# Where the value product stands in an attention kernel: from a fixed two windows behind to wherever a window has room

## The chip, the core and the metric

The kernel runs on one core of a Trainium2 chip. The metric is the time of one execution on the device in microseconds (us); lower is better. Beside the times there is one profiled execution, whose trace gives the start and length of every instruction on each engine: TensorE (PE; its weight loads are listed apart as PEld), VectorE (DVE), ScalarE (ACT), GpSimd (POOL), and SyncE (SP), which issues the DMAs.

## The reference, cut to what matters

```python
def attn(x, Wq, Wk, Wv, Wo):                 # x: 8 x 1024 x 256
    H, G, THETA = 16, 4, 10000.0             # 16 query heads, 4 key heads
    q, k, v = x @ Wq, x @ Wk, x @ Wv
    ...
    scores = jnp.einsum('bhqd,bhkd->bhqk', q, k) / jnp.sqrt(jnp.float32(D))
    p = jax.nn.softmax(scores, axis=-1)
    o = jnp.einsum('bhqk,bhkd->bhqd', p, v)
    return o.transpose(0, 2, 1, 3).reshape(B, S, D) @ Wo

x = x + layernorm(attn(layernorm(x), Wq, Wk, Wv, Wo))
x = x + layernorm(ternary_ffn(layernorm(x)))
```

Queries and keys are rotated by position (RoPE) between the projection and the scores. The feed-forward layer is one product with weights rounded to -1, 0 or 1.

## The kernel before

**Units, groups, blocks.** The work is cut into 16 units of 512 queries (half a sequence). A unit has 4 groups of 4 heads. For a group the keys come in 8 key tiles of 128. A key tile with the 4 heads of a group is a step: four exp scores, one for each head, each 128 keys by 512 queries. So there are 512 steps and 2048 exp scores, counted by `s`. One exp score is one score product into a PSUM bank (`se`, three of them, line 655) and one exp on ACT into an SBUF tile of the pool `ep` (line 671). That pool has 12 tiles. Ahead of that, 13 steps earlier, a second pass over the same scores finds each query's maximum: two score products into a two-bank PSUM tile (`sm`, two of them, line 582), then a maximum over 1024 numbers on DVE (line 607), which may be taken as two halves.

**The value product.** `av_piece` (line 691) multiplies the exp tiles of a key tile with the values and adds up over a group in the one PSUM bank `av`. It works in blocks of 128 query columns, so a key tile has 4 blocks, and there are 2048 blocks, as many as exp scores. A piece is a run of blocks inside one key tile. It costs four weight loads and four matmuls, one for each head, and each 32-bit matmul shows as two instructions in the trace, hence the "x8" there. When a group is finished, `av_out` copies the bank to an SBUF tile of the pool `avp` (5 tiles; ACT, line 704) and sends it to DRAM (`d_av`, line 712).

**Windows.** TensorE, VectorE and ScalarE run an order written out by hand. `window(s)` emits one window: 3 exp scores, or 2 where a part of other work with a PSUM bank of its own is waiting, each beside a score product for the maxima; then the parts that have come due (`do_parts`, at most one banked part in a window of 2, none in a window of 3); then value products. `behind` holds the windows whose value product is still to come, and `av_windows(2)` issues as many blocks as the window two places back had exp scores. So every window ends with 2 or 3 blocks, whatever else it holds. A piece needs all four exp tiles of its key tile.

**Other work.** `P_PARTS` lists by step what projects a later unit (norm, transposes `x`, key and value product `kv_and_dram`, query products `q`, and DMAs through DRAM), `T_PARTS` what follows attention for the unit before (`fetch` of the value products from DRAM, `invert` of the softmax denominators on DVE, `scale` on GpSimd, output product `attn`, feed-forward `ffn`, norms). `P_FIRST` and `T_LAST` replace the steps for the first such unit and the last but one. The DMAs of all of these go through the one queue of SP, in program order; there a DMA that waits holds up those behind it.

Of the kernel before, what the change touches and what calls it, by code (L numbers as in the profile page):

```python
# [16 lines left out]
P = 128  # L17
H = 16
HKV = 4
G = H // HKV  # L20
# [8 lines left out]
def kernel(  # L29
# [35 lines left out]
    NK = S // P  # L65
    UPB = S // UQ
    NU = B * UPB
    NROW = 3 * HD
    SPU = G * NK
    NSTEP = NU * SPU  # L70
    LEAD, START = 13, 10

    const = ctx.enter_context(tc.tile_pool(name="const", bufs=1))
# [1 line left out]
    small = ctx.enter_context(tc.tile_pool(name="small", bufs=4))  # L75
    work = ctx.enter_context(tc.tile_pool(name="work", bufs=2))
    qkp = ctx.enter_context(tc.tile_pool(name="qkp", bufs=1))
    ep = ctx.enter_context(tc.tile_pool(name="ep", bufs=12))
    avp = ctx.enter_context(tc.tile_pool(name="avp", bufs=5))
    tailp = ctx.enter_context(tc.tile_pool(name="tailp", bufs=1))  # L80
    dram = ctx.enter_context(tc.tile_pool(name="dram", bufs=3, space=DRAM))
    ps_mx = ctx.enter_context(tc.tile_pool(name="ps_mx", bufs=2, space=PSUM))
# [110 lines left out]
    ffn = {}  # L193
# [424 lines left out]
    sm, mhl, shifts, reduced, early = {}, {}, {}, [], [None]  # L618
# [30 lines left out]
    es, av_ps, av_sb, d_av = {}, {}, {}, {}  # L649
# [33 lines left out]
    def av_piece(i, first, end):  # L683

        va = v_aug[(i // G // UPB) % 3]
        if first == 0:
            av_ps[0] = ps_av.tile([P, UQ], F32, tag="av", name=f"av_{i}")
        for kt in range(first // UQ, (end - 1) // UQ + 1):
            lo, hi = max(first - kt * UQ, 0), min(end - kt * UQ, UQ)
            for r in (1, 2, 3, 0):  # L690
                nc.tensor.matmul(  # L691
                    av_ps[0][32 * r : 32 * r + 32, lo:hi],
                    va[:, kt, r, :],
                    es[i * NK + kt, r // 2, r % 2][:, lo:hi],
                    start=(kt == 0 and lo == 0),
                    stop=(kt == NK - 1 and hi == UQ),
                )

    def av_out(i):

        u, j = divmod(i, G)
        a = av_sb[u, j] = avp.tile([P, UQ], F32, tag="avsb", name=f"avsb_{i}")
        if i < NU * G - 1:
            nc.scalar.copy(a, av_ps[0])
        else:
            half = UQ // 2
            nc.scalar.copy(a[:, :half], av_ps[0][:, :half])
            nc.vector.tensor_copy(a[:, half:], av_ps[0][:, half:])
        if u < NU - 1:
            if j == 0:  # L710
                d_av[u] = dram.tile([H, 32, UQ], F32, tag="d_av", name=f"d_av_{u}")
            nc.sync.dma_start(out=d_av[u][HKV * j : HKV * (j + 1)], in_=a)


    class Tail:
# [21 lines left out]

        def fetch(self):

            for c in range(2):  # L740
                self.on[c] = self.new("xn", c)
                nc.sync.dma_start(
                    out=self.on[c].rearrange("p t d -> p (t d)"),
                    in_=d_av[self.u][8 * c : 8 * c + 8, 0:HD, :],
                )
            self.den = small.tile([P, UQ // 8], F32, tag="den", name=f"den_{self.u}", bufs=1)
            nc.sync.dma_start(
                out=self.den, in_=d_av[self.u][:, HD, :].rearrange("i (g t) -> i g t", g=8)
            )
# [88 lines left out]
    class LastTail(Tail):  # L838
# [55 lines left out]
        x = o  # L894
# [42 lines left out]
    def load(u):  # L937
# [2 lines left out]


    P_PARTS = (
        (26, "begin", 0), (33, "x", 0, 0), (34, "x", 0, 1), (37, "begin", 1), (43, "x", 1, 0),
        (45, "x", 1, 1), (49, "kv_and_dram"), (51, "q", 0), (52, "kt"), (53, "v"), (55, "q", 1),
        (57, "q_to_dram"),
    )
    L_PARTS = (
        (10, "n", 0), (13, "o", 0), (15, "attn", 0), (16, "stats_a", 0), (19, "stats_x", 0),
# [2 lines left out]
        (29, "attn", 2), (29, "x", 1), (30, "stats_a", 2), (30, "ffn", 1), (31, "stats_f", 1),  # L951
    )
    T_PARTS = (
        (1, "fetch"), (7, "invert"), (8, "scale", 0), (9, "scale", 1), (12, "attn", 0),
        (15, "attn", 1), (15, "stats_a", 0), (17, "stats_a", 1), (19, "stats_x", 0),
        (23, "stats_x", 1), (24, "x", 0, 0), (25, "x", 0, 1), (26, "ffn", 0), (27, "x", 1, 0),
        (29, "x", 1, 1), (31, "ffn", 1), (31, "stats_f", 0), (33, "stats_f", 1),
    )

    P_FIRST = (47, 51, 52, 54, 57, 58, 59, 60, 62, 61, 63, 64)  # L960
    T_LAST = (1, 3, 4, 5, 9, 10, 11, 14, 17, 20, 21, 21, 22, 24, 25, 26, 23, 27)

    warm = []

# [15 lines left out]
    def behind_shift(i, f, *args):  # L980

        with tc.issue_after(shifts[i]):
            f(*args)

    for k, fs in enumerate((
        [second("x", 1, 0), second("x", 1, 1), second("kv", 0)],
        [second("kv", 1), (pick, "q", 0, 0, 1), (pick, "q", 0, 1, 1), second("v"),
         second("rotate_k"), second("split_k")],
        [(pick, "q", 1, 0), (keep_warm, 1)],
        [(keep_warm, 3), second("k"), (keep_warm, 4), (pick, "k", 1, 0), (pick, "k", 1, 1),  # L990
         (keep_warm, 2)],
        [(pick, "q", 1, 1), second("q_product", 0), third("stats", 0),
         third("norm", 0, nc.scalar)],
        [second("q_product", 1), third("stats", 1), third("hi", 0, nc.scalar), third("lo", 0),
         (pick, "q", 2, 0)],
        [(pick, "q", 2, 1), third("norm", 1, nc.scalar), third("hi", 1, nc.scalar),
         third("lo", 1), (keep_warm, 3), (fill_constant_parts, 1)],
        [third("x", 0, 0), (pick, "q", 3, 0), (keep_warm, 3)],
        [third("x", 0, 1), (pick, "q", 3, 1), second("rotate_q", 0), (keep_warm, 2)],
        [third("x", 1, 0), third("x", 1, 1), second("split_q", 0)],  # L1000
        [third("kv_and_dram"), second("rotate_q", 1)],
        [third("v"), second("split_q", 1), second("q_to_dram")],
        [],
        [],
        [(fill_constant_parts, 2)],
        [],
        [third("q", 0)],
        [(behind_shift, 1, third("kt"))],
        [third("q", 1), (behind_shift, 1, stack_queries, 1)],
        [third("q_to_dram")],  # L1010
    )):
        for f in fs:
            at(k - START, *(f if isinstance(f, tuple) else (f,)))
    for u in range(3, NU):
        start = SPU * (u - 4)
        steps = P_FIRST if u == 3 else [k for k, *_ in P_PARTS]
        at(start + steps[0] - 6, load, u)
        if u == 3:
            for k, stage in (
                (7, measure), (9, prepare_wo), (11, add_up), (13, threshold), (15, ternarize),  # L1020
                (22, transpose_ternary),
            ):
                at(k, stage)
        at(start + steps[0] - 1, begin_project, u)
        for k, (_, *p) in zip(steps, P_PARTS):
            at(start + k, part, projects, u, *p)
    for u in range(2, NU):
        at(SPU * (u - 1) + 1, stack_queries, u)
    for u in range(NU - 1):
        start = SPU * (u + 1)  # L1030
        at(start + 1, begin_tail, u)
        steps = [k for k, *_ in T_PARTS] if u < NU - 2 else T_LAST
# [14 lines left out]
        )  # L1047

    REGULAR = 40
    ends = 4 * (NSTEP - LEAD)  # L1050


    ready = []
# [22 lines left out]

    def do_parts(banks):

        while ready:
            f, args = ready[0]  # L1080
            if banked(f, args):
                if banks == 0:
                    break
                banks -= 1
            ready.pop(0)
            f(*args)
            if f is shift_rows:
                split_later.append(args[0])

    def take_low():  # L1090
        while split_later:
# [8 lines left out]
        collect(n)  # L1100
        do_parts(99)

    behind, done, split_later = [], [], []

    def av_windows(lag):

        while len(behind) > lag:
            i, s, size = behind.pop(0)
            first = s % (4 * NK)
            av_piece(i, first * P, (first + size) * P)  # L1110
            if first + size == 4 * NK:
                done.append(i)

    def window(s):


        late, size = s >= ends, window_size(s)
        if done:
            av_out(done.pop())
        if late:  # L1120
            for r2 in range(2):
                exp_two(s // 4, r2)
        else:
            end = min(maxima_by(s + size), 4 * NSTEP)
            for q in range(max(size, end - maxima[0])):
                if q < size:
                    exp_one(s + q)
                if maxima[0] < end:
                    max_scores(maxima[0])
                    maxima[0] += 1  # L1130
                if q == 0:
                    take_low()
            reduce_early(maxima[0])
        take_low()
        behind.append((s // (4 * NK), s, size))
        for n in range(s // 4, (s + size) // 4):
            collect(n)
        do_parts(3 - size if REGULAR <= s < ends else 99)
        av_windows(1 if late else 2)
        return s + size  # L1140

    E = mybir.EngineType
    due, picks = [], []
# [56 lines left out]
    with tc.manual_schedule(engines={E.PE, E.DVE, E.Activation}):  # L1200
        while s < 4 * NSTEP:
            s = window(s)
        av_windows(0)
        av_out(NU * G - 1)
        assert not (todo or due or ready or split_later)
# [70 lines left out]
```

## Time and profile before

| | us |
|---|---|
| median of 3 runs (1644.11 to 1649.19) | 1645.35 |
| profiled execution, its own time | 1642.63 |
| its span, first to last instruction | 1640.8 |

The timeline can be cut into windows: from the first score matmul of one to the first score matmul of the next. Between 105 and 1573 us there are 751, together 1468.8 us. Sorted by what they hold besides scores and value products:

| window (exp scores; part) | windows | all, us | mean length, us | mean blocks | DVE idle in all, us |
|---|---|---|---|---|---|
| light: 3; none | 438 | 791.2 | 1.806 | 2.61 | 97.5 |
| transposes: 2; `x` of either list | 109 | 216.2 | 1.983 | 2.63 | 28.9 |
| heavy: 2; `attn` (31) | 31 | 92.6 | 2.989 | 2.55 | 25.5 |
| heavy: 2; `q` (26) | 26 | 83.8 | 3.225 | 2.50 | 8.4 |
| heavy: 2; `ffn` (28) | 28 | 71.4 | 2.552 | 2.00 | 2.2 |
| heavy: 2; `kv_and_dram` (13) | 13 | 41.8 | 3.212 | 3.00 | 2.8 |
| shift: 2; transpose of the maxima `pm` | 61 | 100.9 | 1.655 | 2.52 | 1.6 |
| rest: 2; small parts or none | 45 | 70.9 | 1.576 | 2.62 | 11.9 |

In the timeline a line gives start, length, engine, line of the kernel, operation, tiles and shape, how many instructions were merged (x8), and in brackets how long the engine had been idle and what ended it. The length of a matmul contains its way through the array, so what a group of matmuls costs the engine is read from its start to the start of the next group.

### The profile page before, as it was taken

The numbers are of one execution on the slowest core, as the hardware profiler recorded it, in microseconds if no ns is written. First come the engines' busy times: TensorE is split into PE (matmuls) and PEld (weight loads), VectorE is DVE, ScalarE is ACT, GpSimd is POOL, SyncE is SP. The second block draws the span as 40 slices with busy tenths as digits, with TensorE's granted clock in tenths as the row PEclk, the third lists the DMA queues.
The fourth block names the chain that finished last, engine by engine and source line by source line (L and its number), as shares of the span: only waits on it lengthen the run. The fifth ranks groups of instructions, "written<-read, shape, count | busy, mean of one in ns | idle before, by whom it ended". The sixth has DMA issues, their size and how long they took to land.

```text
span 1640.8 us, 37250 instructions
## 1 busy us (share of the span) xinstructions
PE 1579.7 (96%) x14712; PEld 818.5 (50%) x14712; DVE 1399.3 (85%) x2049; ACT 1274.8 (78%) x2479; POOL 835.4 (51%) x1239
## 2 busy tenths in 40 slices
PE   7999999999999999999999999999999999999997
PEld 5544455454545545454544545455454544444544
DVE  7778788889898888989889898988989888898964
ACT  4657778878787887878788787887878787877884
POOL 5532457374653737455373835547374552323363
PEclk8989999999999999999999999999999999999999
DMA  4151425125151422515133251513325151231100
GB/s 139 53 101 34 91 77 101 59 76 101 56 106 49 91 67 82 101 46 105 60 83 75 77 106 44 104 49 89 71 67 104 40 97 42 46 70 34 42 15 27
DMA packets 86079, 117.99 MB, mean 72 GB/s; under 512 B 12088, under 2 KB 50808, under 8 KB 85752
## 3 DMA queue, kind: packets, MB, share of 16 engines
q1 hardware_dynamic: 85904, 115.60, 29.9%
q8 instruction: 116, 1.90, 0.5%
q14 instruction: 59, 0.48, 0.1%
HBM read 68.65 MB, written 45.88 MB: 70 GB/s over the span
## 4 chain that ended last, share of the span: by engine, by line
PE 80%; DVE 10%; DMA 3%; ACT 2%; POOL 2%; issue 2%; SPq 1%; POOLq 0%; DVEq 0%; ACTq 0%
PE av L691 28%; PE se L655 28%; PE sm L582 9%; DVE mx L607 7%; PE pa L283 3%; PE pq L283 2%; PE pf L283 2%; PE pt_ot L267 2%; ACT e L671 2%; PE pt_xt L267 2%; PE pkv L283 2%; DMA q_st<-ml 1%; DMA k_rot<-d_k 1%; PE pm L630 1%; DMA dk<-ks 1%
## 5 line engine op out<-in xcount | busy, mean ns | idle before, releaser
L607 DVE TENSOR_REDUCE mx<-sm 128x2 f32<-128x1024 f32 (+1 forms) x1304 | 1205.3, 973 | 191.9 <-PE sm L582 174.1
L671 ACT ACTIVATE e<-se 128x512 f32<-128x512 f32 x1996 | 1058.2, 602 | 223.0 <-PE sm L582 172.4
L582 PE MATMUL sm<-k_st,q_st 64*128 64x512 f32 x2048 | 748.4, 450 | 6.9 <-DVE mx L607 3.9
L655 PE MATMUL se<-q_st,k_st 64*128 64x512 f32 x2048 | 705.5, 441 | 26.7 <-ACT e L671 14.4
L691 PE MATMUL av<-e,v_aug 128*32 128x256 f32 (+3 forms) x8608 | 607.2, 378 | 0.0
L655 PEld LDWEIGHTS se<-q_st,k_st 64*128 64x128 f32 x2048 | 324.9, 185 | 405.7 <-ACT e L671 302.1
L582 PEld LDWEIGHTS sm<-k_st,q_st 64*128 64x128 f32 x2048 | 326.1, 185 | 65.1 <-DVE mx L607 41.9
L691 PEld LDWEIGHTS av<-e,v_aug 128*32 128x32 f32 x8608 | 194.4, 108 | 211.0 <-issue 148.3
L241 POOL TENSOR_SCALAR lnsc<-mv 128x2 f32<-128x2 f32 (+1 forms) x134 | 25.8, 193 | 400.1 <-DVE mv L239 395.1
L765 POOL TENSOR_TENSOR xn<-xn,a 128x512 f32<-128x512 f32 x30 | 38.4, 1282 | 131.8 <-DMA a<-d_rec 101.2
L826 POOL TENSOR_TENSOR a<-a,bias_bc 128x512 f32<-128x512 f32 x30 | 38.6, 1287 | 108.3 <-ACT a L825 108.3
L242 POOL TENSOR_TENSOR lnsc<-lnsc,mhalf 128x2 f32<-128x2 f32 (+1 forms) x134 | 92.5, 691 | 0.9
L162 POOL TENSOR_TENSOR hl<-xn,hl 128x512 fp32r<-128x512 f32 x60 | 76.5, 1287 | 0.4
L253 POOL TENSOR_SCALAR xn<-x,lnsc 128x256 f32<-128x256 f32 x116 | 65.1, 570 | 2.2
L237 DVE BATCH_NORM_STATS2 bnst<-a 128x6 f32<-128x256 f32 x120 | 44.5, 413 | 4.6 <-POOL a L826 4.6
L297 POOL TENSOR_TENSOR t<-q_rot,sin_q_sb 128x512 f32<-128x512 f32 x31 | 39.9, 1288 | 15.5 <-ACT q_rot L439 15.4
L283 PE MATMUL pa<-woh,hl 128*128 128x256 f32 x240 | 46.2, 294 | 1.1 <-ACT e L671 1.1
L283 PE MATMUL pq<-xt,wqkvh 128*128 128x256 f32 x256 | 45.8, 303 | 0.5 <-ACT e L671 0.5
L237 DVE BATCH_NORM_STATS2 bnst<-x 128x6 f32<-128x256 f32 x124 | 45.9, 412 | 0.4 <-DMA x<-in_L_attn_x 0.4
L271 ACT CAST ot<-pt_ot 128x512 fp32r<-128x512 f32 x66 | 39.6, 601 | 4.7 <-PE pt_ot L267 4.7
L439 ACT COPY q_rot<-pq 128x512 f32<-128x512 f32 x32 | 18.8, 586 | 30.9 <-PE pq L283 30.9
L162 POOL TENSOR_TENSOR hlq<-q_rot,hlq 128x512 fp32r<-128x512 f32 x31 | 39.8, 1285 | 4.8 <-ACT hlq L159 4.5
(157 smaller groups left out, 1303.1 us busy)
## 6 DMA issues: line engine op xcount, KB each, us to landing
q_st<-dq SPq DMA_DIRECT2D x90, 256.0 KB
dq<-hlq SPq DMA_DIRECT2D x60, 256.0 KB
d_av<-avsb SPq DMA_DIRECT2D x60, 256.0 KB
x<-in_L_attn_x SPq DMA_DIRECT2D x15, 512.0 KB
xn<-d_av SPq DMA_DIRECT2D x30, 256.0 KB
a<-d_rec SPq DMA_DIRECT2D x30, 256.0 KB
xr<-in_L_attn_x SPq DMA_DIRECT2D x15, 512.0 KB
out_x<-a SPq DMA_DIRECT2D x30, 256.0 KB
```

Source lines behind the costliest of these rows:

```text
L162: eng.tensor_tensor(lo, src, hi.bitcast(F32), ALU.subtract)
L237: nc.vector.bn_stats(st[:, t, :], src[:, t, :])
L242: nc.gpsimd.tensor_tensor(sc[:, 1, :], sc[:, 1, :], mhalf[:, :n], ALU.pow)
L253: eng.tensor_scalar(dst[:, t, :], src[:, t, :], sc[:, 0, t : t + 1] if eng is nc.gpsimd else mv[:, t, 0:1], sc[:, 1, t : t + 1], ALU.add i ...
L267: nc.tensor.transpose(pt[:, c, t * P : (t + 1) * P], src[:, t, c * P : (c + 1) * P], ident_r)
L283: nc.tensor.matmul(out, chunk(left[i], c), chunk(right[j], c), start=(k == 0), stop=(k == len(steps) - 1),)
L297: eng.tensor_tensor(dst, x, table.unsqueeze(1).to_broadcast(list(x.shape)), ALU.mult)
L582: scores = nc.tensor.matmul(sm[0][:, part, :], queries[rows], k_st[(u // UPB) % 3][rows, r2, ch * 512 : (ch + 1) * 512], start=True, stop= ...
L607: early[0] = nc.vector.tensor_reduce(mx[i][:, a, head_and_tile(i, r2, t), lo:n], sm[0][:, lo:n, :], AX.X, ALU.max).ins
L655: nc.tensor.matmul(sc if len(queries.shape) == 2 else sc.rearrange("p (j t) -> p j t", j=G), k_st[(i // G // UPB) % 3][rows, r2, kt * P : ...
L671: nc.scalar.activation(e, sc, AF.Exp, scale=1.0 / D**0.5)
L691: nc.tensor.matmul(av_ps[0][32 * r : 32 * r + 32, lo:hi], va[:, kt, r, :], es[i * NK + kt, r // 2, r % 2][:, lo:hi], start=(kt == 0 and lo ...
```

## The change

The value product is no longer issued at a fixed distance. `behind` and `av_windows` are gone. A counter `av_at` tells how many blocks are done, and at the end of every window `av_end` chooses how far to go: it tries each end up to 8 blocks on, inside the group, and takes the one whose weight (that of the banked parts just issued, plus 21 for each block and 6 for each piece) comes closest to 95, with 45 added for an end inside a key tile. It goes no further than the key tiles whose exps were emitted before this window, and no less far than `least`, which 16 exp tiles need. When the group ends, `av_out` follows in the next window as before.

With it go: 16 exp tiles for 12 and 2 output tiles for 5; `fetch` two steps later; several project parts up to five steps later, and the DMAs of `kt` and `q_to_dram` held behind the latest DMA of shift rows; for the last but one unit `fetch`, `invert` and both `scale` two steps later. A window's number of exp scores, its parts and the order inside it are as before.

```diff
+    E_TILES = 16
-    ep = ctx.enter_context(tc.tile_pool(name="ep", bufs=12))
-    avp = ctx.enter_context(tc.tile_pool(name="avp", bufs=5))
+    ep = ctx.enter_context(tc.tile_pool(name="ep", bufs=E_TILES))
+    avp = ctx.enter_context(tc.tile_pool(name="avp", bufs=2))
...
     P_PARTS = (
-        (26, "begin", 0), (33, "x", 0, 0), (34, "x", 0, 1), (37, "begin", 1), (43, "x", 1, 0),
-        (45, "x", 1, 1), (49, "kv_and_dram"), (51, "q", 0), (52, "kt"), (53, "v"), (55, "q", 1),
-        (57, "q_to_dram"),
+        (30, "begin", 0), (35, "x", 0, 0), (36, "x", 0, 1), (37, "begin", 1), (43, "x", 1, 0),
+        (45, "x", 1, 1), (49, "kv_and_dram"), (51, "q", 0), (54, "kt"), (53, "v"), (55, "q", 1),
+        (62, "q_to_dram"),
     )
...
     T_PARTS = (
-        (1, "fetch"), (7, "invert"), (8, "scale", 0), (9, "scale", 1), (12, "attn", 0),
+        (3, "fetch"), (7, "invert"), (8, "scale", 0), (9, "scale", 1), (12, "attn", 0),
...
-    T_LAST = (1, 3, 4, 5, 9, 10, 11, 14, 17, 20, 21, 21, 22, 24, 25, 26, 23, 27)
+    T_LAST = (3, 5, 6, 7, 9, 10, 11, 14, 17, 20, 21, 21, 22, 24, 25, 26, 23, 27)
...
+    def behind_latest(f, *args):
+
+        behind_shift(max(shifts), f, *args)
...
-        at(start + steps[0] - 1, begin_project, u)
-        for k, (_, *p) in zip(steps, P_PARTS):
-            at(start + k, part, projects, u, *p)
+        first = 25 if u == 4 else steps[0]
+        at(start + first, begin_project, u)
+        for k, (_, *p) in zip([first + (u == 4), *steps[1:]], P_PARTS):
+            behind = [behind_latest] if p[0] in ("kt", "q_to_dram") else []
+            at(start + k, *behind, part, projects, u, *p)
...
+    GAP, COLUMNS, PIECE, SPLIT = 95, 21, 6, 45
+    WEIGHT = {"x": 46, "v": 33, "ffn": 112, "q": 162, "attn": 162, "kv_and_dram": 162}
...
+    def av_end(s, size, weight):
+
+
+
+        at = av_at[0]
+        least = (s + 3 - E_TILES + 3) // 4 * 4
+        then = (s - 1) // 4 * 4
+        best = None
+        for end in range(at, min(at + 8, at // (4 * NK) * 4 * NK + 4 * NK) + 1):
+            if end > max(at, least) and (end + 3) // 4 * 4 > s - size - 1:
+                break
+            pieces = (end + 3) // 4 - at // 4 if end > at else 0
+            rest = abs(weight + COLUMNS * (end - at) + PIECE * pieces - GAP)
+            rest += SPLIT * (end % 4 > 0) + 1000 * max(0, least - end)
+            if not ready and end > at and end == then:
+                rest += 80
+            if best is None or rest < best[0]:
+                best = rest, end
+        return best[1]
...
-        behind.append((s // (4 * NK), s, size))
         for n in range(s // 4, (s + size) // 4):
             collect(n)
-        do_parts(3 - size if REGULAR <= s < ends else 99)
-        av_windows(1 if late else 2)
-        return s + size
+        weight = do_parts(3 - size if REGULAR <= s < ends else 99)
+        s += size
+        av_until(s - 4 if late else av_end(s, size, weight))
+        return s
```

`do_parts` now returns the summed weight of the banked parts it issued (those of `WEIGHT`, 30 for another part, 25 for the shift rows' transpose and the like), and `av_until(end)` issues the blocks from `av_at` to `end` by `av_piece`.

More of the change, by code (lines that the diff above doesn't have):

```diff
@@ L738, in fetch @@
         def fetch(self):
+            assert (self.u, G - 1) in av_sb
             for c in range(2):
@@ L1077, in do_parts @@
     def do_parts(banks):
+        weight = 0
         while ready:
@@ L1084, in do_parts @@
                 banks -= 1
+                weight += WEIGHT.get(args[2], 30) if f is part else 25
             ready.pop(0)
@@ L1088, in do_parts @@
                 split_later.append(args[0])
+        return weight
     def take_low():
@@ L1101, in start_step, with av_until @@
         do_parts(99)
[L1103 to L1111, printed above, removed]
-                done.append(i)
+    done, split_later, av_at = [], [], [0]
+    def av_until(end):
+        i, first = divmod(av_at[0], 4 * NK)
+        last = min(end - i * 4 * NK, 4 * NK)
+        if last > first:
+            av_piece(i, first * P, last * P)
+            av_at[0] += last - first
+            if last == 4 * NK:
+                done.append(i)
+    def av_end(s, size, weight):
[14 more added lines that the diff above has]
+        return best[1]
     def window(s):
@@ L1202 @@
             s = window(s)
-        av_windows(0)
-        av_out(NU * G - 1)
-        assert not (todo or due or ready or split_later)
+        av_until(s)
+        av_out(done.pop())
+        assert av_at[0] == s and not (todo or due or ready or split_later or done)
     spare[0] = 1
```

## The prediction

> **What bounds the kernel now.** I read the page first: the engines' shares and the costliest groups.
>
> ```profile
> PE 1579.7 (96%) x14712; PEld 818.5 (50%) x14712; DVE 1399.3 (85%) x2049; ACT 1274.8 (78%) x2479; POOL 835.4 (51%) x1239
> ...
> L607 DVE TENSOR_REDUCE mx<-sm 128x2 f32<-128x1024 f32 (+1 forms) x1304 | 1205.3, 973 | 191.9 <-PE sm L582 174.1
> L671 ACT ACTIVATE e<-se 128x512 f32<-128x512 f32 x1996 | 1058.2, 602 | 223.0 <-PE sm L582 172.4
> ...
> L691 PE MATMUL av<-e,v_aug 128*32 128x256 f32 (+3 forms) x8608 | 607.2, 378 | 0.0
> ```
>
> PE looks full and DVE waits mostly for PE, but a busy matmul is not PE at its peak. So I went to the sums by stretch (length; then busy time and instructions of PE, PEld, DVE, ACT, POOL; clock, DMA share, GB/s): a window with an `attn` part, a light one, the steady state.
>
> ```profile
> 602.72:605.58 2.86, 2.86 (x29) 1.95 (x25) 1.29 (x2) 1.64 (x4) 0.00 (x0) 1.00 0.02 6
> ...
> 608.74:610.59 1.85, 1.85 (x19) 0.82 (x15) 1.85 (x4) 1.85 (x5) 0.00 (x0) 1.00 0.00 0
> 120.00:1570.00 1450.00, 1416.80 (x13642) 723.59 (x13634) 1273.73 (x1829) 1163.93 (x2260) 739.03 (x1077) 1.00 0.31 72
> ```
>
> The heavy window is PE's alone: DVE is busy 1.29 of 2.86 us. In the light one DVE and ACT are busy throughout. The timeline shows both inside.
>
> ```profile
> 605.01 0.64 PE L691 MATMUL av<-e,v_aug 128*32 128x256 f32 x8
> ...
> 605.58 0.50 PE L655 MATMUL se<-q_st,k_st 64*128 64x512 f32 x1
> ...
> 609.08 0.39 PE L655 MATMUL se<-q_st,k_st 64*128 64x512 f32 x1
> 609.36 0.18 PEld L582 LDWEIGHTS sm<-k_st,q_st 64*128 64x128 f32 x1 [0.23 <-DVE mx L607]
> ```
>
> A score product for exps and one for maxima normally start together, on two halves of the array. At 609.36 the second waits for DVE to give back an `sm` bank, starts 0.28 us after its partner, and the pair no longer runs as one. So light windows are held by DVE and heavy ones by PE, and neither engine uses the other's slack: the two `sm` tiles carry it about one maximum ahead.
>
> **What a window needs of PE.** Start to start, the shortest of each kind: three score pairs 0.89 us, two pairs 0.66; an `attn`, `q` or `kv` product 1.62, `ffn` 1.10, a transposes part 0.445, the maxima's transpose 0.215. A value piece:
>
> ```profile
> 598.31 0.85 PE L691 MATMUL av<-e,v_aug 128*32 128x384 f32 x8
> 599.10 0.49 PE L655 MATMUL se<-q_st,k_st 64*128 64x512 f32 x1
> ```
>
> ```profile
> 1589.33 1.06 PE L691 MATMUL av<-e,v_aug 128*32 128x512 f32 x8
> 1590.32 0.73 PE L655 MATMUL se<-q_st,k_st 64*128 64x512 f32 x4
> ```
>
> 2 blocks take 605.58 - 605.01 = 0.57 us, 3 take 0.78 (median of 165), 4 take 0.996 (median of 9). That is 0.2135 us a block plus 0.142 us for each time PE turns to the value product. Splitting the blocks into two pieces within one turn hardly costs: 1 + 2 blocks in two pieces take 0.788 us against 0.783 in one.
>
> With these the 751 windows of the table need 1328.9 us of PE and last 1468.8: 140 us is waiting, 94 of it in light windows (438 need 697.3, last 791.2), 19 in those with transposes, 16 in heavy ones, 11 in the others.
>
> **The change, part 1: fewer turns.** I put the rule of `av_end` through the windows in the order of the trace of before. Heavy windows weigh 112 or more, over the goal of 95, and get no block (98 of 98). Light ones: 4 blocks weigh 90, so 301 of 438 take a whole key tile, 27 take 3, 39 take 2, and 71 only 1, where no finished tile is left. Transposes windows (46): 28 with 4, 40 with 2, 41 with none. Windows with the maxima's transpose (25): 3 or 4. So 611 windows have a value product where all 751 had: 140 turns x 0.142 = 20 us of PE less. The need is 1308.6 us. By class: light 697 to 759, heavy 274 to 209, transposes 197 to 171, maxima 95 to 107, rest 66 to 63.
>
> The Trainium skill ("TensorEngine Tiling (Array Packing)", Instruction Overhead) gives every matmul about 60 cycles of overhead. From about 1000 steady pieces the change goes to 611, eight instructions each, 3100 fewer; at 2.4 GHz that would be an estimated 78 us. The rows above deny it: eight more instructions in a turn cost 0.005 us, so I price turns, not instructions.
>
> **Part 2: the waits.** Back to back, a maximum over 1024 takes DVE 1.13 us (median start to start of 492), so a light window asks 1.5 x 1.13 = 1.70 us of it, plus whatever norms fall there. PE's need with 4 blocks is 0.89 + 0.996 = 1.886, above that; with 3 it was 1.675, with 2 1.46, below. Low bound of the waiting in light windows: only those with fewer than 4 blocks wait, 27 x 0.03 + 39 x 0.24 + 71 x 0.45 = 42 us. High bound: it stays at 94. The nearest rows where PE needs more than DVE are the windows with the maxima's transpose (1.56 us against 1.13): 6 us of waiting in 61. That speaks for the low end; but a margin of 0.19 is thin and the norms' 150 us of DVE (1273.7 less some 970 maxima at 1.16, between 1.13 whole and 1.20 in halves) come in lumps. I take the middle, 68: 26 us less.
>
> **Part 3: what gets worse.** A transposes window without blocks needs 1.105 us of PE, but ACT has two exps at 0.49 and a copy of 0.59 there, 1.57: 41 x 0.46 = 19 us, or 0 where the three `se` banks let PE run on. I take 10. In heavy windows DVE must do its backlog elsewhere; I keep their 16 us of waiting (that is rival 1's subject).
>
> **Part 4: DMAs and buffers.** `fetch` goes on SP two steps (6 us) later, `invert` stays.
>
> ```profile
> 280.51 0.34 SPq L712 DMA_DIRECT2D d_av<-avsb  x1
> 281.68 0.40 SPq L836 DMA_DIRECT2D out_x<-a  x1
> 288.81 0.67 SPq L742 DMA_DIRECT2D xn<-d_av  x1
> 289.54 0.58 SPq L747 DMA_DIRECT2D den<-d_av  x1
> 290.21 0.54 SPq L836 DMA_DIRECT2D out_x<-a  x1
> 293.81 1.38 SPq L646 DMA_DIRECT2D q_st<-ml  x2
> ```
>
> ```profile
> 201.25 0.55 DVE L752 RECIPROCAL den<-den 128x64 f32<-128x64 f32 x1 [2.10 <-DMA den<-d_av]
> ```
>
> Already now `fetch` sits on SP until `d_av` has landed, 8 us after the copy's DMA; the step it is listed at isn't what sets it. In this unit the reciprocal ran at 298.26 without waiting; in the one that waited, the denominators came 3.4 us after their DMA (issued 197.84), so here at about 293, with 5 us in hand. The trail after a window becomes 3 to 8 blocks, so the group's copy comes up to some 4 blocks x 0.756 us (1468.8 us for 1942 blocks) = 3 us later. Cost 0, since those 5 us cover it. Without that cover the reciprocal holds the maxima behind it on DVE's queue, and PE by `sm`; the shift rows (`q_st<-ml`) behind `fetch` on SP have 293.81 - 290.21, 3 us. The later `begin` leaves POOL 5 steps (15 us) before its transposes, for some 4 us of work: 0, or 3 us a unit (one step) were it one step late. `kt` and `q_to_dram` go behind the shift rows' DMA on SP, with units of time before their use: 0. Two output tiles instead of five: a tile is used again two groups (48 us) later, its DMA has landed after 8: 0. For the last unit but one, `invert` and `scale` come 6 us later: POOL was done at 1549.65 and `attn` began at 1552.99, so it is 2.7 us late, once.
>
> **Sum.** -20 - 26 + 10 + 3 = -33 us on the profiled 1642.6: 1610. The median of the runs lies 2.7 us above it: 1612. With the ends of each term: -20 - 52 + 0 + 0 = -72 (1573) to -20 + 0 + 19 + 3 = +2 (1647).
>
> **Rivals.** 1. *DVE is the bound, and only its idle time can be saved.* In the 98 heavy windows DVE is idle for 39 us alone (table): the 65 us that leave them were mostly used by it for backlog and norms. If this work moves to light windows, the gain is at most 39 us, and 301 light windows with 0.19 us of new idle time can eat all of it: 1640 to 1645. For it: the `ffn` and `kv` windows, 0.08 and 0.22 us idle each. Against it: the same backlog exists because light windows ask more of DVE than PE takes; when they are longer, it shrinks.
>
> 2. *Late denominators, slower.* Place: the reciprocal at the head of DVE's queue. Each us that the copy, `d_av`, `fetch` chain is later than the 5 us in hand stops DVE, then PE, 14 times. Above 33 / 14 = 2.4 us it decides; at 4 us it costs 56, and the time is 1645 + 23 = 1668. For it: the reciprocal did wait once, 2.1 us. Against: 3 us of delay against 5.
>
> 3. *The rule doesn't do what it says:* too few whole tiles are finished, pieces stay as they are: 1645. Against it: the count above, 359 of 611 turns with a whole tile.
>
> **How the numbers follow.** The forecast gets 0.64. Rival 1 gets 0.18, spread over a little faster (0.05), no change (0.08) and a little slower (0.05), rival 2 0.14, rival 3 0.04, half no change, half slower. No change means within 0.3%, 4.9 us, about what a measurement here can tell. Faster: 0.64 + 0.05 = 0.69; same 0.08 + 0.02 = 0.10; slower 0.21. The forecast's own range is 1573 to 1647; the whole range reaches toward rival 2 and gives up a little of the far gain: 1576 to 1660.
>
> **What would show it.** Right: some 4900 steady value matmuls instead of 8000, most with 512 columns; heavy windows about 2.3 us; light ones about 1.9 with score pairs starting together; DVE's idle time before its maxima less by some 25 us in sum. Wrong: light windows of 2 us and more with `sm` waiting for DVE (rival 1); idle time before the reciprocal ended by its DMA (rival 2); many value products of 1 or 2 blocks (rival 3). What makes the prediction wrong soonest is the split of light waits, 42 to 94.

## The result and the profile after

The changed kernel takes 1650.63 us (median of 20 runs, 1646.7 to 1654.12), the kernel before 1645.48 (20 runs). The ratio is 1.0032, 95% interval 1.0022 to 1.0041: slower by a third of a percent, where 2% faster was forecast. The profiled execution has a span of 1646.3 us.

The page of the changed kernel, shares and costliest groups (its lines lie one or two further down: 608 is the maximum, 656 and 583 the score products, 672 the exp, 692 the value product):

```profile
PE 1586.6 (96%) x11152; PEld 715.1 (43%) x11152; DVE 1410.6 (86%) x2037; ACT 1262.9 (77%) x2479; POOL 831.8 (51%) x1239
...
L608 DVE TENSOR_REDUCE mx<-sm 128x2 f32<-128x1024 f32 (+1 forms) x1292 | 1218.7, 982 | 185.6 <-PE sm L583 166.7
L672 ACT ACTIVATE e<-se 128x512 f32<-128x512 f32 x1996 | 1058.5, 602 | 236.0 <-PE sm L583 206.5
...
L692 PE MATMUL av<-e,v_aug 128*32 128x512 f32 (+3 forms) x5048 | 574.1, 526 | 0.0
```

Its value products, by form (count, then busy us and mean ns):

```profile
L692 PE MATMUL av<-e,v_aug 128*32 128x512 f32 x3144 | 422.0, 608 | 0.0
L692 PE MATMUL av<-e,v_aug 128*32 128x384 f32 x736 | 78.4, 498 | 0.0
L692 PE MATMUL av<-e,v_aug 128*32 128x128 f32 x736 | 39.4, 286 | 0.0
L692 PE MATMUL av<-e,v_aug 128*32 128x256 f32 x432 | 34.5, 391 | 0.0
```

So the change does what it says: 3144 of 5048 value matmuls now cover a whole key tile, and there are 3560 fewer. Cut into the same 751 windows as before, with TensorE's need priced as in the prediction:

| windows | all, us: before, after | need | waiting (all - need) | DVE idle |
|---|---|---|---|---|
| light, 438 | 791.2, 900.0 | 697.3, 761.0 | 93.8, 139.0 | 97.5, 74.5 |
| heavy, 98 | 289.6, 217.8 | 273.7, 208.9 | 15.8, 9.0 | 38.9, 24.4 |
| transposes, 109 | 216.2, 177.5 | 197.2, 164.5 | 19.0, 13.0 | 28.9, 49.4 |
| shift, 61 | 100.9, 110.9 | 94.9, 109.1 | 6.0, 1.8 | 1.6, 13.2 |
| rest, 45 | 70.8, 70.4 | 65.6, 62.8 | 5.2, 7.6 | 11.9, 14.2 |
| all, 751 | 1468.8, 1476.6 | 1328.9, 1306.2 | 139.9, 170.4 | 178.7, 175.8 |

The need fell by 22.7 us. The waiting grew by 30.5 us, nearly all in light windows. Two views show where. First the stretches (length, busy us of PE, PEld, DVE, ACT, POOL): the heavy window is as short as it was meant to be, 1.63 us from its product to the next scores.

```profile
607.69:609.32 1.63, 1.60 (x12) 1.49 (x13) 1.22 (x1) 0.88 (x2) 0.00 (x0) 1.00 0.02 5
602.61:604.49 1.88, 1.88 (x15) 0.55 (x14) 1.70 (x3) 1.19 (x3) 1.88 (x3) 1.00 0.00 0
```

Then the timeline of the light window that follows another `attn` product (start, length, in brackets the idle time and what ended it):

```profile
617.64 0.49 PE L656 MATMUL se<-q_st,k_st 64*128 64x512 f32 x1
...
617.79 0.58 ACT L794 COPY a<-pa 128x512 f32<-128x512 f32 x1 [0.82 <-issue]
...
617.98 0.39 PE L656 MATMUL se<-q_st,k_st 64*128 64x512 f32 x1
...
618.27 1.58 ACT L672 ACTIVATE e<-se 128x512 f32<-128x512 f32 x3
618.43 0.18 PEld L656 LDWEIGHTS se<-q_st,k_st 64*128 64x128 f32 x1 [0.49 <-ACT a L794]
618.43 0.49 PE L656 MATMUL se<-q_st,k_st 64*128 64x512 f32 x1
```

The result of `attn` lies in one of the three `se` banks. Two score products fit into the other two. The third needs the bank of the result, which ScalarE copies from 617.79 to 618.37. It starts at 618.43, 0.45 us after the second; the usual step after the second pair is 0.23. Before the change two or three value blocks stood between the product and the next scores, and ScalarE copied under them (ScalarE in the trace of before, beside the blocks at 605.01 and the scores at 605.58):

```profile
605.16 0.59 ACT L792 COPY a<-pa 128x512 f32<-128x512 f32 x1 [0.81 <-issue]
```

To weigh this over the whole run I took every run of score products that lasts over 0.06 us more than the shortest of its length, and put the excess down to the wait that ended last in it, in us between 105 and 1573 us:

| kernel | VectorE (`sm`) | exps (`se`) | ScalarE's copies of parts (`se`) | other |
|---|---|---|---|---|
| before | 73.6 | 41.7 | 0.8 | 6.1 |
| after | 75.0 | 32.2 | 33.6 | 6.9 |

The copies are a new wait of 33 us. It eats up the 22.7 us of need and the 9.5 us that the exps got back. (8.6 of these 9.5 us are 14 transposes parts that waited for their bank in the kernel before; experiment 8 comes back to them.)

Because these terms nearly cancel, one single wait weighs much. At the start of the 61st score run the changed kernel is 1.3 us ahead of the kernel before (175.8 us for 177.0), and fifteen windows later 3.4 us behind (210.5 for 207.1); in the 1300 us that follow it loses only 2 us more. Inside these fifteen windows lie one wait of TensorE and the 7 us behind it (the last three numbers of a stretch are the clock, the DMA share and GB/s), first before, then after the change:

```profile
201.56 0.46 PE L655 MATMUL se<-q_st,k_st 64*128 64x512 f32 x1 [3.06 <-DMA q_st<-ml]
201.60:208.40 6.80, 6.75 (x68) 3.26 (x72) 6.18 (x9) 5.83 (x12) 0.00 (x0) 1.00 0.31 102
```

```profile
202.68 0.76 PE L656 MATMUL se<-q_st,k_st 64*128 64x512 f32 x1 [4.83 <-DMA q_st<-ml]
202.30:209.00 6.70, 6.32 (x32) 2.84 (x34) 4.23 (x5) 3.73 (x7) 0.19 (x1) 0.50 0.43 146
```

TensorE waits for the DMA of the shift rows, which stands on SP right behind the two DMAs of `fetch`: it is issued at 199.60 us, before the change at 198.55. Behind the longer wait the granted clock is 0.50 for some 7 us, where it was 1.00 in the kernel before. This is one execution of each kernel; what the place costs in the others is not shown. (The kernel `most_before` of experiment 8, with the old `fetch`, also waits there, 3.6 us, and has a clock of 0.50 for some 7 us.)

### The profile page after: what moved, and what is told of

The parts are those of the page before. It is cut to its first block, busy times and chain, and to the rows that moved or that the text cites. A ratio compares the mean times of both kernels' runs of the same rounds, so it can differ in the third digit from the quotient of the medians.

```text
span 1646.3 us, 30056 instructions
## 1 busy us (share of the span) xinstructions
PE 1586.6 (96%) x11152; PEld 715.1 (43%) x11152; DVE 1410.6 (86%) x2037; ACT 1262.9 (77%) x2479; POOL 831.8 (51%) x1239
## 4 chain that ended last, share of the span: by engine, by line
PE 73%; DVE 10%; POOL 5%; issue 5%; ACT 4%; DMA 3%; SPq 0%; POOLq 0%; DVEq 0%; ACTq 0%
PE se L656 27%; PE av L692 26%; PE sm L583 8%; DVE mx L608 7%; PE pq L284 3%; PE pt_ot L268 2%; PE pa L284 2%; DVE bnst L238 2%; PE pf L284 1%; PE pkv L284 1%; ACT a L827 1%; PE pt_xt L268 1%; ACT a L794 1%; ACT e L672 1%; PE pm L631 1%
## 5 line engine op out<-in xcount | busy, mean ns | idle before, releaser
L608 DVE TENSOR_REDUCE mx<-sm 128x2 f32<-128x1024 f32 (+1 forms) x1292 | 1218.7, 982 | 185.6 <-PE sm L583 166.7
L583 PE MATMUL sm<-k_st,q_st 64*128 64x512 f32 x2048 | 773.7, 453 | 8.8 <-DVE mx L608 6.3
L656 PE MATMUL se<-q_st,k_st 64*128 64x512 f32 x2048 | 751.0, 450 | 26.1 <-ACT e L672 9.0
L692 PE MATMUL av<-e,v_aug 128*32 128x512 f32 (+3 forms) x5048 | 574.1, 526 | 0.0
L692 PEld LDWEIGHTS av<-e,v_aug 128*32 128x32 f32 x5048 | 99.8, 108 | 162.9 <-issue 141.0
L705 ACT COPY avsb<-av 128x512 f32<-128x512 f32 x63 | 36.9, 586 | 17.5 <-PE av L692 15.9
L238 DVE BATCH_NORM_STATS2 bnst<-a 128x6 f32<-128x256 f32 x120 | 44.6, 413 | 4.4 <-POOL a L828 4.4
L272 ACT CAST xt<-pt_xt 128x512 fp32r<-128x512 f32 x64 | 38.1, 602 | 4.2 <-PE pt_xt L268 4.1
```

Source lines behind the costliest of these rows:

```text
L238: nc.vector.bn_stats(st[:, t, :], src[:, t, :])
L583: scores = nc.tensor.matmul(sm[0][:, part, :], queries[rows], k_st[(u // UPB) % 3][rows, r2, ch * 512 : (ch + 1) * 512], start=True, stop= ...
L608: early[0] = nc.vector.tensor_reduce(mx[i][:, a, head_and_tile(i, r2, t), lo:n], sm[0][:, lo:n, :], AX.X, ALU.max).ins
L656: nc.tensor.matmul(sc if len(queries.shape) == 2 else sc.rearrange("p (j t) -> p j t", j=G), k_st[(i // G // UPB) % 3][rows, r2, kt * P : ...
L692: nc.tensor.matmul(av_ps[0][32 * r : 32 * r + 32, lo:hi], va[:, kt, r, :], es[i * NK + kt, r // 2, r % 2][:, lo:hi], start=(kt == 0 and lo ...
```

## The experiments

The theories: A, VectorE sets the pace, and what left the heavy windows was cover for its backlog (rival 1). B, long runs of blocks keep TensorE from refilling VectorE's banks. C, the placement pays and the moved steps lose it. D, the value piece was the cover for ScalarE's copy. E and F divide C between the project steps and the rest, G and H come later. All ratios are to the kernel before, timed beside them.

**1. Only the moved steps and buffers (`old_place`).** Value product two windows behind again:

```diff
-        weight = do_parts(3 - size if REGULAR <= s < ends else 99)
-        s += size
-        av_until(s - 4 if late else av_end(s, size, weight))
-        return s
+        behind.append(s + size)
+        do_parts(3 - size if REGULAR <= s < ends else 99)
+        av_windows(1 if late else 2)
+        return s + size
...
+    def av_windows(lag):
+
+        while len(behind) > lag:
+            av_until(behind.pop(0))
```

> The changed kernel, with the value product put back to two windows behind; its 16 exp tiles, 2 output tiles and all moved steps stay. Theory A (VectorE sets the pace: work that left the heavy windows on TensorE was hiding VectorE's backlog) and theory B (a run of four blocks on end keeps TensorE from refilling VectorE's score banks): the moved steps are free, 1643 to 1649 us, ratio to before 0.998 to 1.002. Theory C (the placement pays, the moved steps and buffers lose it again): 1660 us or more, since the placement's own gain would be missing.

1653.88 us, ratio 1.0048 (1.0031 to 1.0065), against all three: the moved steps aren't free for the old placement, but the placement hardly pays either (the changed kernel stands at 1.0032, and the intervals overlap).

**2. VectorE relieved, in both kernels (`half_before`, `half_after`).**

```diff
-                mx[i][:, ::-1, head_and_tile(i, r2, t), ch], sm[0], AX.X, ALU.max
+                mx[i][:, ::-1, head_and_tile(i, r2, t), ch], sm[0][:, :, :256], AX.X, ALU.max
...
-            mx[i][:, a, head_and_tile(i, r2, t), lo:n], sm[0][:, lo:n, :], AX.X, ALU.max
+            mx[i][:, a, head_and_tile(i, r2, t), lo:n], sm[0][:, lo:n, :256], AX.X, ALU.max
```

> The kernel before, with each maximum taken over half of its score columns (the shift of the softmax then comes from half of the keys). A whole maximum then costs VectorE about 0.6 us in place of 1.13. Theory A and B: VectorE is no longer late, the 140 us of waiting in the steady windows shrink to some 30 to 60, and the time to some 1540 to 1570 us. Theory C says nothing of it. If VectorE were not what light windows wait for: no more than 20 us faster.

> The changed kernel with the same half maxima. Theory A: with VectorE out of the way TensorE's need decides, and the changed kernel is 15 to 30 us below the half_before run (1306 us of need in place of 1329). Theory B: the same or somewhat less gain. Theory C: no gain over half_before, or a loss.

1585.79 us (0.9640, 0.9622 to 0.9658) and 1608.85 us (0.9766, 0.9741 to 0.9791). VectorE is worth 60 us to the kernel before, somewhat less than expected. But with VectorE out of the way the change loses 23 us, where theory A wanted a gain. So what the change loses here isn't VectorE's. The waits in the score runs of these two: VectorE 2.0 and 0.9 us, exps 55.2 and 50.8, ScalarE's copies 0.6 and 44.6. That is theory D: 44 us of new waits against 22.7 of need.

**3. Two turns in a light window (`split_turn`).** Half of the blocks after the second score pair:

```diff
+                if two and q == 1:
+                    av_until(av_at[0] + (goal - av_at[0]) // 2)
...
-        av_until(s - 4 if late else av_end(s, size, weight))
+        av_until(s - 4 if late else goal if two else av_end(s, size, weight))
```

> The changed kernel, but a light window gives half of its blocks after its second score pair and the rest at its end: two turns in place of one, 0.14 us more of TensorE each. Theory A: VectorE sets the pace of light windows, TensorE has 0.3 us to spare there: 1645 to 1655 us, VectorE's idle time in light windows (0.17 us each) hardly moves. Theory B: the idle time of VectorE in light windows falls to under 0.1 us, light windows from 2.05 to 1.95 us or less, 1605 to 1625 us. Theory C: no change against the changed kernel.

1716.63 us, 1.0435 (1.0415 to 1.0455): no theory had it. Between 103 and 1650 us there are 948 turns where the changed kernel has 599, and 1075 score runs for 751. At 0.142 us a turn and 0.2 a further score run (two pairs 0.66 and one 0.433 in place of three in 0.892) that is 50 + 65 = 115 us of need, of which 71 show (the stretch is 1547.3 us for 1476.6). So most of it was paid although light windows were said to have 0.3 us to spare: here the waiting inside score runs was mostly no slack that work between the runs could fill. Theory B's 1605 to 1625 us was missed by far, but an edit that costs 115 us of its own doesn't settle B. What speaks against B is experiment 2: with VectorE relieved it expected a gain too, and the change lost 23 us.

**4. Two blocks behind each part, where finished tiles allow (`cover`, `half_cover`).**

```diff
-        return best[1]
+        end = best[1]
+        if weight >= 46 and end == at and s >= REGULAR and at % (4 * NK) < 4 * NK - 1:
+            if (at + 2 + 3) // 4 * 4 <= s - size - 1:
+                end = at + 2
+        return end
```

> The changed kernel, but a window with a part whose result ScalarE copies (attn, q, kv, ffn, transposes) takes 2 blocks where the rule gave it none, if finished tiles allow. Theory D (the value piece after such a part was the cover under which ScalarE copied the part's bank; without it the third score product of the next window waits for that bank): the 30 to 36 us of score products waiting for ScalarE's copies in the changed kernel go, up to 139 more turns cost 20 us at most, 1630 to 1640 us. Theory A (VectorE sets the pace, whatever stands after the part): the blocks only change windows, 1645 to 1652 us.

> The same two blocks with half maxima (each maximum over half of its score columns). Theory D: against half_after (1609) the 44 us of waits for copies go and 20 us of turns come, 1580 to 1592 us. Theory A: VectorE is out of the way in both, so only the turns show: 1615 to 1630 us.

1649.47 us, 1.0030 (1.0018 to 1.0042), and 1603.90 us, 0.9751 (0.9730 to 0.9772). Neither is what D expected, and the traces say why: light windows had used up the finished tiles. The `kv_and_dram` windows still have no block, `attn` and `q` windows 1.1 and 1.0 on average, and the waits for copies only fall to 27 us in both (from 33.6 and 44.6). The test was too weak to decide.

**5. The project steps of before (`old_place_old_steps`, `old_steps`).** `P_PARTS` and the loop that places it as in the kernel before; the first on top of `old_place`, the second on the changed kernel:

```diff
-        (30, "begin", 0), (35, "x", 0, 0), (36, "x", 0, 1), (37, "begin", 1), (43, "x", 1, 0),
-        (45, "x", 1, 1), (49, "kv_and_dram"), (51, "q", 0), (54, "kt"), (53, "v"), (55, "q", 1),
-        (62, "q_to_dram"),
+        (26, "begin", 0), (33, "x", 0, 0), (34, "x", 0, 1), (37, "begin", 1), (43, "x", 1, 0),
+        (45, "x", 1, 1), (49, "kv_and_dram"), (51, "q", 0), (52, "kt"), (53, "v"), (55, "q", 1),
+        (57, "q_to_dram"),
...
-            behind = [behind_latest] if p[0] in ("kt", "q_to_dram") else []
-            at(start + k, *behind, part, projects, u, *p)
+            at(start + k, part, projects, u, *p)
```

> The changed kernel with the value product two windows behind as before, and with the project steps (and the place of the kt and q_to_dram DMAs) of before too. Still changed: 16 exp tiles, 2 output tiles, fetch two steps later, the last but one unit's steps. Theory E (the moved project steps are what old_place lost, 8.6 us): 1643 to 1648 us. Theory F (fetch, buffers or the last unit's steps): 1650 us or more.

> The changed kernel with the project steps of before, value product placed as changed. Theory E: 1640 to 1645 us, 6 to 9 us below the changed kernel. Theory F: 1648 to 1653 us, as the changed kernel.

1648.12 us, 1.0022 (1.0006 to 1.0038), and 1677.23 us, 1.0194 (1.0171 to 1.0217). Under the old placement the project steps may account for half of the loss; the intervals of `old_place` and this one overlap. Under the new placement the moved steps are worth 27 us, the other way round from E. The view of waits, the one line of TensorE waiting for the DMA of the shift rows (us in all, times, longest), in the changed kernel and in `old_steps`:

```profile
PE se L656 <- DMA q_st<-ml: 8.7, 3, 4.8
```

```profile
PE se L656 <- DMA q_st<-ml: 29.7, 16, 4.4
```

Score products for exps can't start before the shift rows have landed. With the old steps TensorE waits for that DMA 16 times. What holds it on SP can be seen at one of these places in `old_steps` (the DMA issues, then the scores):

```profile
544.81 3.02 SPq L431 DMA_DIRECT2D dk<-ks  x4
548.11 3.57 SPq L482 DMA_DIRECT2D k_st<-dk  x6
551.78 1.41 SPq L647 DMA_DIRECT2D q_st<-ml  x2
553.89 0.54 PE L656 MATMUL se<-q_st,k_st 64*128 64x512 f32 x1 [2.66 <-DMA q_st<-ml]
```

The DMAs of `kt` go first; they waited for GpSimd's `ks` until 544.8 us. In the changed kernel they are held behind the shift rows. The waits account for 21 of the 27 us. The rest isn't taken apart, but the granted clock is lower too: 0.977 in the mean for 0.987, and in the stretch from 553.9 to 557.6 us, right behind this wait, 0.54.

**6. Fewer blocks in light windows, one behind every part (`half_thin`, `thin`).** To give `cover` the tiles it lacked:

```diff
-    GAP, COLUMNS, PIECE, SPLIT = 95, 21, 6, 45
+    GAP, COLUMNS, PIECE, SPLIT = 75, 21, 6, 0
...
+        if weight >= 46 and end == at and s >= REGULAR:
+            if (at + 1 + 3) // 4 * 4 <= s - size - 1:
+                end = at + 1
```

> Half maxima (each maximum over half of its score columns), the changed rule with a goal of 75 and nothing added for an end inside a key tile, and at least one block after any part that ScalarE copies. Counted through the rule, light windows then take 3 blocks (4 in 88), and each of the 207 windows with such a part has a piece, 751 turns as before. Theory D (the piece behind a part covers ScalarE's copy of its bank): the 44 us of score products waiting for copies in half_after go, 20 us of turns come back: 1580 to 1590 us, at the level of half_before (1586). Theory G (long runs of blocks or the moved steps are what costs, not the missing cover): 1605 to 1630 us.

> The same rule with whole maxima. Theory D: the 30 to 36 us of waits for copies go, 20 us of turns come back: 1630 to 1642 us, at or below the kernel before. Theory G: 1650 to 1665 us. Theory A (VectorE sets the pace either way): 1645 to 1652 us.

With half maxima 1586.69 us, 0.9651 (0.9626 to 0.9676): 22 us below `half_after` and level with `half_before`, as D has it. The edit also makes the runs of blocks in light windows shorter, 3 for 4, so the time alone doesn't separate D from G; the waits do. The waits for copies are down from 44.6 to 6.6 us, with all 16 exp tiles, moved steps and a need of 1328.2 us. In the view of waits of the two, the score products' weight loads for three of the copies (this view counts idle time of the weight loads, also some under running matmuls) stand in `half_after`

```profile
PEld se L656 <- ACT a L827: 17.6, 29, 0.8
PEld se L656 <- ACT q_rot L440: 12.9, 27, 0.8
...
PEld se L656 <- ACT kv_t L359: 5.8, 13, 0.4
```

and in `half_thin` of these three the first alone is left with more than one us:

```profile
PEld se L656 <- ACT a L827: 7.7, 29, 0.8
```

With whole maxima `thin` took 1654.78 us, 1.0070 (1.0051 to 1.0088), though the waits for copies went there too, from 33.6 to 7.3 us. The need came back (1306 to 1328), waits for exps rose from 32.2 to 49.0 (experiment 8 says which), those for VectorE stayed (75.0, 71.4).

**7. Two exp scores after a part without blocks (`half_next_two`, `next_two`).**

```diff
-        size = min(2 if s >= REGULAR and any(banked(*p) for p in ready) else 3, left, ends - s)
+        short = s >= REGULAR and (bare[0] or any(banked(*p) for p in ready))
+        size = min(2 if short else 3, left, ends - s)
...
+        bare[0] = weight >= 33 and av_at[0] == was
```

> Half maxima, value product placed as changed, but the window after one whose part was left without blocks has two exp scores in place of three, so it needs no third bank while ScalarE copies the part. Theory D: waits for copies fall from 44 us to under 15, the shorter windows cost some 16 us of TensorE (a pair 0.33 us in a window of two, 0.297 in one of three, and up to 46 more turns): 1585 to 1597 us. Theory G: no wait goes, 1615 to 1630 us.

> The same with whole maxima. Theory D: 1632 to 1645 us. Theory G or A: 1650 to 1668 us.

1645.39 us, 1.0007 (0.9992 to 1.0023), and 1684.47 us, 1.0241 (1.0210 to 1.0271), worse than every theory. The waits for copies are nearly gone, but the windows' new rhythm brings others: in `next_two` TensorE waits for the shift rows' DMA

```profile
PE se L656 <- DMA q_st<-ml: 40.1, 16, 3.6
```

and in `half_next_two` VectorE stands 13 times, 43.7 us in all, before statistics that GpSimd's sum hasn't yet reached. The test moved too much to speak for or against D.

**8. VectorE an eighth lighter (`most_before`, `most_after`, `most_thin`).** Open was why the cover pays with half maxima and not with whole ones. Theory H: with whole maxima VectorE's pace takes the place of the wait removed. The edit is that of 2, with `:448` for `:256`.

> The kernel before with each maximum taken over 448 of its 512 columns, an eighth less work for VectorE. Theory H (with whole maxima VectorE's pace takes the place of whatever wait is removed; a little lighter, it no longer does): 1605 to 1625 us.

> The changed kernel with the same maxima over 448 columns. Theory H: the copies of parts now decide, as with half maxima: 1618 to 1638 us, 8 us or more above most_before. If nothing but VectorE's pace separated the two placements: within 4 us of most_before.

> The kernel thin (a piece behind each copied part, 3 blocks in light windows) with maxima over 448 columns. Theory H: 6 us or more below most_after, 1605 to 1625 us. Otherwise: 2 to 6 us above most_after, as thin stands to the changed kernel with whole maxima.

1608.70 us (0.9777, 0.9761 to 0.9792), 1619.85 us (0.9840, 0.9826 to 0.9854), 1601.42 us (0.9728, 0.9712 to 0.9743). With an eighth less of VectorE's work on the maxima the order is another: `most_thin` is 18 us below the changed placement and 7 below the one of before, where with whole maxima `thin` was the slowest of the three. All by the waits in score runs:

| kernel | need of the steady windows | VectorE | exps | copies | other |
|---|---|---|---|---|---|
| half_before | 1328.9 | 2.0 | 55.2 | 0.6 | 8.9 |
| half_after | 1306.2 | 0.9 | 50.8 | 44.6 | 7.8 |
| half_thin | 1328.2 | 4.0 | 40.1 | 6.6 | 6.5 |
| most_before | 1328.9 | 27.8 | 42.5 | 0.5 | 10.9 |
| most_after | 1306.2 | 26.2 | 41.9 | 44.4 | 7.7 |
| most_thin | 1328.2 | 35.1 | 29.5 | 8.7 | 4.7 |
| thin | 1328.2 | 71.4 | 49.0 | 7.3 | 3.6 |

The order came as H has it (the time of `most_thin` lies just below its range), and yet it doesn't show H, since the kernels differ in one more thing. In `thin` a transposes part that stands in the window behind a transpose of the maxima starts only when ScalarE has ended the first exp of its own window:

```profile
604.79 1.09 ACT L672 ACTIVATE e<-se 128x512 f32<-128x512 f32 x2 [0.24 <-PE sm L583]
605.53 0.50 PE L268 MATMUL pt_xt<-ident_r,xs 128*128 128x128 f32 x4 [0.54 <-ACT e L672]
```

The view of waits has this in `thin` 38 times, in the kernel before 14 times,

```profile
PE pt_xt L268 <- ACT e L672: 13.0, 24, 0.5
PE pt_ot L268 <- ACT e L672: 7.5, 14, 0.5
```

```profile
PE pt_ot L267 <- ACT e L671: 6.9, 14, 0.5
```

and not once in the changed kernel or in any kernel of the table but `thin`. The programs built from the kernels say why: these 38 and 14 parts were given the PSUM bank of that first exp, the same parts in the changed kernel and the other kernels of the table the bank of the maxima's transpose one window earlier. Why the banks are given out differently is open; `thin` and `most_thin` differ in nothing but the columns of the maxima. The score runs before these parts last 0.62 us over the shortest (some 0.2 us in `most_thin`), in all 23.4 us in `thin` and 8.6 us in the kernel before. Both sums stand under the exps (49.0 and 41.7). Taken off in full, the most that they can be worth, they leave an estimated 1631 us for `thin` and 1637 for the kernel before, against 1651 for the changed one: the order of the kernels with 448 columns.

So the missing cover is shown as the loss with 256 and with 448 columns: there the copies are 44 us of waits, and a piece behind every part takes most of them away and 22 and 18 us off the time. With whole maxima the copies' 33.6 us of waits are shown as well, but that the cover pays there rests on the estimate. That VectorE's load decides whether the cover pays (H) isn't shown.

**A version that beats both.** `half_before` and `half_thin` (1586 us, 3.5% faster) and `most_thin` beat both kernels, nearly all of it by their maxima and not by the placement (`most_thin` is 7 us below `most_before`). They take the shift of the softmax from part of the keys. In exact arithmetic the softmax doesn't depend on the shift; what is given up is the guarantee that no exponent is above zero.

## Why the prediction was wrong

**Fewer turns: right.** 611 turns were counted, 599 came; the need was to fall by 20 us and fell by 22.7. Heavy windows with `q` and `kv_and_dram` last 2.32 and 2.28 us, as their parts add up to. The Trainium skill ("TensorEngine Tiling (Array Packing)", Instruction Overhead) would have given the fewer matmuls a price of their own, an estimated 78 us; the need, priced by turns alone, accounts for the `q`, `kv_and_dram` and `ffn` windows to 0.04 us (`attn` windows last 0.25 us longer than theirs), and a run of 4 blocks still takes the 0.996 us of before (median of 390), so no such price shows. The same page (Key Properties) says that a change of tiling mode drains TensorE. That fits a fixed 0.142 us for each turn; no run here shows the drain by itself.

**The waits: the step that failed.** "I take the middle, 68" for the waiting in light windows, where 94 had been measured: it became 139. I had looked at light windows as a balance of TensorE's and VectorE's need and asked only whether 1.886 us is more than 1.70. What reaches into them from the window before wasn't in the sum. The step "in heavy windows ... I keep their 16 us of waiting" is right for those windows (9.0) and misses the point: the value piece behind a part was priced as TensorE work alone, and it was the cover of ScalarE's copy, whose bank the next window's third score product needs. 33.6 us of score runs wait there, 14.0 of them behind transposes without blocks. For the transposes the copy was named in the sum, 10 us, but looked for inside the window, where the waiting fell (19 to 13). A piece put back behind each part takes most of these waits away (with half maxima from 44.6 to 6.6 us, experiment 6).

**Light windows don't relax by being longer.** Waits for VectorE were to shrink there by up to half. They stayed (73.6 and 75.0 us in the score runs), since VectorE's busy time in light windows rose from 694 to 826 us with what had been done in heavy ones. This is rival 1's mechanism, and its sentence on the 65 us that VectorE mostly used holds: VectorE's idle time in all windows went from 178.7 to 175.8. So the 26 us that the forecast took off for light windows didn't come, even apart from the copies. But rival 1 put the end at 1640 to 1645 and made VectorE the only cause; with VectorE relieved the change lost even more, 23 us (experiment 2).

**DMAs and buffers: right in all units but one, wrong by omission.** "Cost 0, since those 5 us cover it" holds in all units but one. Where the reciprocal had already waited 2.1 us there was no cover: it waited 4.2 us, and TensorE 4.83 us for 3.06 for the shift rows behind `fetch`, with the lower clock after it. Rival 2's mechanism is there, once: some 4.7 us, nearly the whole measured difference of the profiled spans (5.5 us), though the spread of the other executions isn't known. For the last unit but one the output product waited for GpSimd, as priced (2.7 us; ScalarE's copy of it stood 2.7 us for GpSimd's split). The moved project steps were priced at 0 each. With the new placement they're worth 27 us (experiment 5): without them TensorE waits 21 us longer for the shift rows' DMA, behind the DMAs of `kt` where it was looked at.

**Rival 3** is ruled out by the forms above. The measured 1650.6 lies inside the whole range (1576 to 1660) and outside the forecast's own (1573 to 1647), on the side that got 0.21. That it ends so near the kernel before is luck: 22.7 us less need and 9 us from other banks nearly cancel 33 us of copies and one wait of some 5 us.

## What to carry to other kernels

When a piece of work is moved, ask what ran under it on the other engines, not only what it costs on its own: here 0.57 us of TensorE were the time in which ScalarE emptied a bank of a ring of three. A saving of need is worth its length only if no ring hands it back, so follow each bank of the ring to its next user in the window behind. And when two kernels that should differ in one thing come out against a theory, see first whether their parts still wait for the same things: here 38 parts had been given another bank.

## What was not expected

An eighth less reduction work (448 of 512 columns) took 37 us off the kernel before (at most 8.6 of them by the other banks), and the remaining cut to 256 columns only 23 more. Waiting inside score runs was little reserve: 115 us of extra need put between the score pairs cost 71 us. The place of a few small DMAs in one queue was worth more than the whole change: the same project steps cost at most some microseconds under one placement of the value product and 27 us under the other.
